# SyncE's loads in program order, head additions one VectorE operation later, and a head step inside a layer's first pair of chunks, in a Fourier-operator kernel

## The chip, the cores and the metric

The kernel runs on one core of one Trainium2 chip. The metric is the device time of one execution in microseconds, the median over the runs shown. One more execution was profiled; every duration in this document that is not called a run's time comes from such a profile.

## The reference

The input is `x`, eight images of 8 channels and 256x256 pixels. The work per image is a group norm, a Fourier neural operator of four layers with a two-matrix head, a residual addition, a second group norm, a 3x3 maximum filter and a second residual addition. Cut to what is computed:

```python
def _spectral_conv(x, w1, w2):
    xf = jnp.fft.rfft2(x).reshape(Bb, G, WID, Hh, Wf)
    lo = jnp.einsum('bgixy,gioxy->bgoxy', xf[:, :, :, :M1, :M2], w1c)
    hi = jnp.einsum('bgixy,gioxy->bgoxy', xf[:, :, :, Hh - M1:, :M2], w2c)
    return jnp.fft.irfft2(out_ft.reshape(Bb, G * WID, Hh, Wf), s=(Hh, Ww))
...
h = _gconv1x1(h, fc0_w, fc0_b)
for i in range(4):
    h1 = _spectral_conv(h, sp_w1[i], sp_w2[i])
    h2 = _gconv1x1(h, w_w[i], w_b[i])
    h = h1 + h2
    if i < 3:
        h = _gswish(h, betas[i])
h = _gswish(_gconv1x1(h, fc1_w, fc1_b), betas[3])
return _gconv1x1(h, fc2_w, fc2_b)
...
x = x + _L0_conv_ref(_gn(x), ...)
x = x + _L1_conv_ref(_gn(x))      # 3x3 maximum, border -2
```

There are 4 groups (G) of 10 channels (WID), 12 by 12 modes kept at both ends of the rows, and a hidden width of 128 per group.

## The kernel before

The state of an image, `h`, stays in SBUF as 11 chunks (NCH). A layer works on it in stages, each a Python generator that yields where work of another stage may be put in:

- `spectrum_h` (layers 1 to 3): four VectorE transposes T0 to T3 (L353), then the matmuls `p_b` (L362) and six short VectorE products into `B` (L369).
- `mix`: twelve VectorE operations, alternately a product (L390) and a sum (L393) over the spectral weights `t` (tag `sw`, two buffers, loaded by `load_sw`, L379); two subtractions and additions into `F` (L405, L406); the matmuls `p_f` (L415); and one VectorE multiply with the mask `own` that spreads the sums into `fz` (L428).
- `rows_of`: the matmuls `p_g` (L447 or L452) in three parts and copies into `zt` (L204).
- `layer`: for each chunk a `burst` of matmuls `p_z` (L523 or L526, then L529) that ScalarE turns into `h` (L534), the VectorE transposes `turn` (L477), the matmuls `p_d` (`transform`, L494) and `p_u` (`gather`, L508). Chunks go in pairs k = 0 to 5. In layer 3 there are only bursts (L536), and each chunk is stored to DRAM (L538).

The head of image b runs while the layers of image b+1 run: it is cut into 128 steps. A step is `first` (four groups of matmuls L686 and two SiLUs, L687 and L688); odd steps add a `second` (matmuls L708 that sum into a PSUM tile `acc`) and a VectorE addition of `acc` to the output rows `y` (L713, L711 where rb is 0). Each element of a yielded tuple, `(1,)` or `(1, 1)`, is one step. A yielded "tail" gives one piece of the 3x3 filter (`dilate`) of the image before. In layer 3 the spectrum and the mix of the next image's layer 0 are taken in pieces too (`start`, through `next(side)`); what is left of that mix follows after the yield "stored".

[...]the tag `one` has two slots of one bank, and `tri` two slots of three. A step's `first` takes a slot of each, and `acc`, `p_f`, `p_b` and `p_u` take one of `one`.

TensorE, VectorE and ScalarE run in the order in which the program is written (`manual_schedule`). The DMAs on SyncE's queue (SP) are placed by a planner: the 44 loads `h<-in_xp` of layer 0 (`read_x`, L542), the weights (L379), the head's `hs<-stored` (L678), the rows `y` (L701), the stores (L538) and `load_x` (L74). Until image 0 has been stored no head runs (`alone`).

Of the kernel before, what the change touches and what calls it, by code (L numbers as in the profile page):

```python
# [19 lines left out]
HW = 256  # L20
NPIX = HW * HW
G = 4
# [21 lines left out]
def fno_dilate_kernel(ctx: ExitStack, tc: tile.TileContext, a: dict, out: bass.AP):  # L44
    nc = tc.nc
    mm = nc.tensor.matmul
    PE, DVE, ACT = mybir.EngineType.PE, mybir.EngineType.DVE, mybir.EngineType.Activation

# [74 lines left out]
    nc.vector.memset(fz, 0.0)  # L123
    own = const.tile([128, NQ], F32, tag="own", name="own")
    nc.vector.memset(own, 0.0)
    for i in range(NQ):
        nc.vector.memset(own[part(i), i : i + 1], 1.0)

# [218 lines left out]
    def spectrum_h(b, l, out_):  # L347

        rows = turned.rearrange("p t f -> p (t f)")[:, : NBLK * WID * 128]
        view = rows.rearrange("p (g i k) -> p i g k", g=G, k=32)  # L350
        for g in range(G):

            nc.vector.transpose(  # L353
                rows[:, 960 * g : 960 * (g + 1)].rearrange("p (i r) -> p i r", r=32), windows(g))
            yield (1,) if g < G - 1 else (1, 1)
        p = ps_a(f"p_b_{b}_{l}")
        for k in range(2):
            for n in range(2 * NBLK):
# [16 lines left out]
        out_["bt"] = bt  # L375
# [6 lines left out]
    def mix(b, l, out_):  # L382
# [3 lines left out]
        for n in range(12):  # L386
            k, k2 = n // 4, n // 2 % 2
            pr = turned[:, 2, 1024 * k2 : 1024 * k2 + 800].rearrange("p (g m i) -> p g m i", g=G, i=WID)
            if n % 2 == 0:
                nc.vector.tensor_tensor(  # L390
                    pr, sw[k], bt[:, k2, k].unsqueeze(2).to_broadcast([128, G, 2 * WID, WID]), ALU.mult)
            else:
                nc.vector.tensor_reduce(  # L393
                    s[k2][:, k].rearrange("p g s o -> p (g s o)"),
                    pr.rearrange("p g m i -> p (g m) i"), AX.X, ALU.add,
                )
            if n == 3:
                sw.append(load_sw(l, 2))
            if l > 0:
                if n not in (2, 6, 10):  # L400
                    yield (1,)
            elif n % 2 or n > 7:
                yield (1,)
        f = sb.tile([128, 2, 3, G, WID], F32, tag="F", bufs=1, name=f"F_{b}_{l}")
        nc.vector.tensor_tensor(f[:, 0], s[0][:, :, :, 0, :], s[1][:, :, :, 1, :], ALU.subtract)  # L405
        nc.vector.tensor_tensor(f[:, 1], s[0][:, :, :, 1, :], s[1][:, :, :, 0, :], ALU.add)  # L406
        if l == 0:
            yield (1,)

        p = ps_a(f"p_f_{b}_{l}")  # L410
        sums = p[:, : 6 * WID * G].rearrange("p (o g s k) -> p s o g k", o=WID, g=G, s=2)
        for slot in range(2):
            for n, (table, part_of) in enumerate(((0, slot), (1 + slot, 1 - slot))):
                for q in range(4):
                    mm(sums[part(q), slot], fold[part(q), table, :],  # L415
                       f[part(q), part_of].rearrange("p k g o -> p o g k"), start=n == 0, stop=n == 1)
        nc.vector.tensor_copy(fz[0:32, :, :, 24], cz[:, l])
# [8 lines left out]
        if l < 2:  # L426
            nc.vector.tensor_copy(fz[0:32, :, :, 25], cz[:, 4 if l == 0 else 3])
        nc.vector.tensor_tensor(  # L428
            fz[:, :, :, : 6 * NQ].rearrange("p o g (q k) -> p (o g) q k", q=NQ),
            p[:, : 6 * WID * G].rearrange("p (n k) -> p n k", k=6).unsqueeze(2).to_broadcast([128, WID * G, NQ, 6]),  # L430
            own.unsqueeze(1).unsqueeze(3).to_broadcast([128, WID * G, NQ, 6]), ALU.mult)

    def rows_of(b, l, side):
# [3 lines left out]
        for os_ in (range(0, 4), range(4, 8), range(8, 10)):  # L437
# [16 lines left out]
            for u, o in enumerate(os_):  # L454
# [7 lines left out]
                copy(u, dst, src)  # L462
            yield (1, 1) if os_[0] == 0 or os_[0] == 8 and l < 3 else (1,)
            if l < 3:
                yield "tail"
            elif os_[0] != 4:
                next(side, None)


    def layer(b, l, out_, stored, side):  # L470
# [68 lines left out]

        def read_x(c):  # L540
            for g in range(G):
                nc.sync.dma_start(  # L542
                    h[32 * g : 32 * g + 6, c].rearrange("p f w -> p (f w)"), a["xp"][b, c, g])

        if l == 0:
            for c in range(NCH):
                read_x(c)
            wcn = sb.tile([128, 32], F32, tag="wcn", bufs=1, name=f"wcn_{b}")
            nc.vector.tensor_scalar(wcn, wc, out_["mr"][:, 1:2], None, ALU.mult)
        if l == 3:  # L550
            for c in range(NCH):
# [6 lines left out]
                if c in (0, 1, 2, 5, 6, 7):  # L558
                    yield "tail"
                next(side, None)  # L560
            return
        for k in range((NCH + 1) // 2):
# [3 lines left out]
            if k > 1:  # L566
                gather(k - 2)
            if k == 0 or alone[0]:
                turn(c)
# [94 lines left out]


    def head(b, stored, stats):
        hs, acts, box = {}, {}, {}
# [5 lines left out]
        def load_state(k):  # L673

            if k < NQ * NCH:
                j, c = k // NCH, k % NCH
                hs[k] = sb.tile([128, PIX], F32, tag="hs", bufs=4, name=f"hs_{b}_{k}")
                nc.sync.dma_start(hs[k], stored[c][:, PIX * j : PIX * (j + 1)])  # L678

        def first(n):  # L680
# [10 lines left out]
        def second(n):  # L691

            t, rb = n // 16, n % 16
            if rb == 0:
                if last:
                    y = ya[:, 1 + 2 * t : 3 + 2 * t, 1 : HW + 1]
                else:
                    y = sb.tile([128, 512], F32, tag="yp", name=f"y_{b}_{t}")
                    y = y.rearrange("p (s w) -> p s w", s=2)
                box["y"] = y  # L700
                nc.sync.dma_start(  # L701
                    y, a["x"][b].rearrange("c (p t s w) -> (c p) t s w", p=16, t=8, s=2)[:, t])
            y, acc = box["y"], ps_a(f"p_fc2_{b}_{n}")
            sums = acc.rearrange("p (s w) -> p s w", s=2)
            for i in range(2):
                act = acts.pop(n + i)
                for g in range(G):
                    mm(acc[part(g), :], w2[:, g, 15 - rb - i : 47 - rb - i], act[:, g, :],  # L708
                       start=i == 0, stop=i == 1)
            if rb == 0:  # L710
                nc.vector.scalar_tensor_tensor(y, sums, b2, y, ALU.add, ALU.add)  # L711
# [11 lines left out]

        load_state(0)
        load_state(1)
        yield
        for n in range(STEPS):
# [5 lines left out]
            yield  # L733
        second(STEPS - 2)


# [38 lines left out]

    heads, tails, count = [], [], [0]

    def step():
# [8 lines left out]
        count[0] += 1  # L787
        return True
# [5 lines left out]
    stats_of = {}  # L794
    with tc.manual_schedule(engines={PE, DVE, ACT}):
        d = {}
        for _ in start(0, d):
            pass
        for b in range(n_img):
            stored = [dram.tile([128, NQ * PIX], F32, tag=f"hs{c}", name=f"stored_{b}_{c}") for c in range(NCH)]  # L800
            ahead = {}
            for n in layers(b, stored, d, start(b + 1, ahead)):
                if n == "stored":
                    if b + 1 < n_img:
                        stats_of[b] = sb.tile([128, 8, 6], F32, tag="bn_y", name=f"bn_y{b}")
                    else:
                        stats_of[b] = spare[:, 16384:16480].rearrange("p (n s) -> p n s", s=6)
                    heads.append((b, head(b, stored, stats_of[b])))
                    next(heads[-1][1])
                    alone[0] = False  # L810
                elif n == "tail":
                    tail()
                elif heads:
                    for _ in n:
                        step()
            d = ahead
        while step():
            tail()
        for t in tails:
# [165 lines left out]
```

## Time and profile before

| | us |
|---|---|
| median of 3 runs | 3972.9 (3970.92 to 3978.73) |
| profiled execution, its own time | 3984.03 |
| its span, first to last instruction | 3982.2 |
| TensorE busy | 3689.1 |
| ScalarE busy | 2829.6 |
| VectorE busy | 2443.7 |
| mean granted TensorE clock | 0.960 |

The profiled execution took 11 us more than the median of the runs. An engine's busy time is a sum over stages with different limits, so the table says only where to look first: which wait ends last in a stage is read from the timeline of that stage. One image takes 484.6 us in the steady part: the second mix's `p_f` of two successive images start at 1430.29 and 1914.92 us.

### The profile page before, as it was taken

The numbers are of one execution on the slowest core, as the hardware profiler recorded it, in microseconds if no ns is written. First come the engines' busy times: TensorE is split into PE (matmuls) and PEld (weight loads), VectorE is DVE, ScalarE is ACT, GpSimd is POOL, SyncE is SP. The second block draws the span as 40 slices with busy tenths as digits, with TensorE's granted clock in tenths as the row PEclk, the third lists the DMA queues.
The fourth block names the chain that finished last, engine by engine and source line by source line (L and its number), as shares of the span: only waits on it lengthen the run. The fifth ranks groups of instructions, "written<-read, shape, count | busy, mean of one in ns | idle before, by whom it ended". The sixth has DMA issues, their size and how long they took to land.

```text
span 3982.2 us, 116980 instructions
## 1 busy us (share of the span) xinstructions
PE 3689.1 (93%) x53114; PEld 1427.5 (36%) x53114; DVE 2443.7 (61%) x3675; ACT 2829.6 (71%) x2923; POOL 116.9 (3%) x202
## 2 busy tenths in 40 slices
PE   5669999999999999999999999999999989999997
PEld 2334333333333333333333333333333333333222
DVE  6665665466675666756666566665666556764643
ACT  3336777767777677776777767777777767778886
POOL 1000000000000000000000000000000000000000
PEclk8879999999999999999999999999999989999998
DMA  3014111432125221261213611135112542115321
GB/s 86 15 47 173 51 41 35 164 95 63 59 85 176 62 61 57 80 212 33 63 54 94 198 36 60 56 123 167 56 43 58 163 121 59 56 44 188 110 70 47
DMA packets 114121, 344.94 MB, mean 87 GB/s; under 512 B 16040, under 2 KB 18536, under 8 KB 98200
## 3 DMA queue, kind: packets, MB, share of 16 engines
q1 hardware_dynamic: 95432, 276.32, 22.3%
q0 software_dynamic: 18192, 61.13, 4.7%
q8 instruction: 418, 6.85, 0.7%
q14 instruction: 79, 0.65, 0.1%
HBM read 213.39 MB, written 123.74 MB: 85 GB/s over the span
## 4 chain that ended last, share of the span: by engine, by line
PE 79%; DVE 11%; issue 4%; ACT 4%; DMA 3%; SPq 0%; POOL 0%; DVEq 0%; POOLq 0%; ACTq 0%
PE p_fc L686 22%; PE p_fc L708 21%; PE p_z L529 9%; PE p_d L494 7%; PE p_z L526 6%; PE p_z L523 3%; PE p_u L508 3%; PE p_b L362 2%; DVE turned L477 2%; PE p_g L452 2%; PE p_g L447 2%; PE p_f L415 2%; DVE turned L353 1%; DVE turned L390 1%; DMA t<-in_spw 1%
## 5 line engine op out<-in xcount | busy, mean ns | idle before, releaser
L688 ACT ACTIVATE act<-p_fc 128x1536 f32<-128x1536 f32 x1024 | 1491.2, 1456 | 1.4 <-PE p_fc L686 1.4
L686 PE MATMUL p_fc<-hs,c_w 32*128 32x512 f32 x8192 | 1183.1, 644 | 49.1 <-DVE y L713 22.0
L708 PE MATMUL p_fc<-act,c_w 128*32 128x512 f32 x8192 | 1003.2, 606 | 5.1 <-ACT act L687 4.7
L687 ACT ACTIVATE act<-p_fc 128x512 f32<-128x512 f32 x1024 | 615.1, 601 | 494.2 <-PE p_fc L686 479.4
L477 DVE STREAM_TRANSPOSE turned<-h 128x1024 f32<-128x1024 f32 x528 | 630.3, 1225 | 322.6 <-ACT h L534 322.4
L534 ACT ACTIVATE h<-p_z 128x512 f32<-128x512 f32 (+1 forms) x528 | 511.8, 1021 | 293.1 <-PE p_z L529 293.1
L713 DVE TENSOR_TENSOR y<-p_fc,y 128x512 f32<-128x512 f32 x392 | 268.2, 684 | 569.8 <-PE p_fc L708 569.6
L686 PEld LDWEIGHTS p_fc<-hs,c_w 32*128 32x128 f32 x8192 | 379.5, 187 | 628.4 <-ACT act L687 226.9
L708 PEld LDWEIGHTS p_fc<-act,c_w 128*32 128x32 f32 x8192 | 216.7, 110 | 733.8 <-issue 366.2
L529 PE MATMUL p_z<-c_binv,zt 32*128 32x256 f32 x5632 | 422.1, 415 | 0.0
L529 PEld LDWEIGHTS p_z<-c_binv,zt 32*128 32x128 f32 x5632 | 264.3, 191 | 318.1 <-issue 305.0
L526 PE MATMUL p_z<-h,c_wt 32*32 32x512 f32 x8448 | 353.5, 599 | 6.2 <-ACT act L687 4.1
L494 PE MATMUL p_d<-turned,c_fw 32*32 32x480 f32 (+1 forms) x9216 | 312.2, 541 | 20.9 <-DVE turned L477 20.6
L498 ACT ACTIVATE turned<-p_d 128x1440 f32<-128x1440 f32 x144 | 183.1, 1271 | 101.7 <-PE p_d L494 98.5
L536 ACT ACTIVATE h<-p_z,c_bias 128x512 f32<-128x512 f32 (+1 forms) x176 | 186.6, 1111 | 71.0 <-PE p_z L529 70.8
L204 DVE COPY zt<-p_g 128x264 f32<-128x264 f32 x300 | 161.9, 617 | 95.2 <-PE p_g L447 42.4
L494 PEld LDWEIGHTS p_d<-turned,c_fw 32*32 32x32 f32 x9216 | 129.3, 103 | 201.7 <-issue 66.8
L390 DVE TENSOR_TENSOR turned<-t,B 128x800 f32<-128x800 f32 x192 | 188.5, 982 | 20.5 <-DMA t<-in_spw 20.4
L393 DVE TENSOR_REDUCE S<-turned 128x80 f32<-128x800 f32 x192 | 189.0, 984 | 5.7
L353 DVE STREAM_TRANSPOSE turned<-zt 128x960 f32<-128x960 f32 x96 | 177.4, 1874 | 2.5
L415 PE MATMUL p_f<-F,c_fold 32*32 32x120 f32 x1024 | 62.1, 391 | 102.7 <-DVE F L405 86.9
L526 PEld LDWEIGHTS p_z<-h,c_wt 32*32 32x32 f32 x8448 | 94.1, 103 | 163.5 <-ACT act L687 59.8
(180 smaller groups left out, 1997.2 us busy)
## 6 DMA issues: line engine op xcount, KB each, us to landing
stored<-h SPq DMA_DIRECT2D x88, 1024.0 KB
hs<-stored SPq DMA_DIRECT2D x352, 256.0 KB
t<-in_spw SPq DMA_DIRECT2D x96, 400.0 KB
yin<-y_rows POOLq DMA_DIRECT2D x56, 512.0 KB, 5.0
h<-in_xp SPq DMA_DIRECT2D x352, 48.0 KB
turned<-in_xw SPq DMA_DIRECT2D x16, 1024.0 KB
y<-in_x SPq DMA_DIRECT2D x56, 256.0 KB
y_rows<-y POOLq DMA_DIRECT2D x56, 256.0 KB, 2.3
```

Source lines behind the costliest of these rows:

```text
L353: nc.vector.transpose(rows[:, 960 * g : 960 * (g + 1)].rearrange("p (i r) -> p i r", r=32), windows(g))
L390: nc.vector.tensor_tensor(pr, sw[k], bt[:, k2, k].unsqueeze(2).to_broadcast([128, G, 2 * WID, WID]), ALU.mult)
L477: nc.vector.transpose(dst[:, 2 * i : 2 * i + 2], h[:, c, 2 * i : 2 * i + 2].rearrange("p f (s x) -> p f s x", s=2))
L494: mm(banks[q][part(v % 4), : 240 * n], fw8[part(q), v, :], t[part(q), :, :, v, : NBLK * WID], start=v < 4, stop=v >= 4)
L526: mm(o, wt[part(q), l, g, :], h[part(q), c, f, :], start=True, stop=False)
L529: mm(banks[q][:, HW * s : HW * (s + 1)], zt[part(q), 2 * c + s].rearrange("p f o -> p (f o)"), binv[part(q), :], start=False, stop=s == 1)
L534: nc.scalar.activation(dst, src, AF.Silu)
L686: mm(banks[g], w1[part(g), blk, :], hs[k][part(g), :], start=True, stop=True)
L687: nc.scalar.activation(act[:, 0, :], one, AF.Silu)
L688: nc.scalar.activation(act[:, 1:4, :], tri, AF.Silu)
L708: mm(acc[part(g), :], w2[:, g, 15 - rb - i : 47 - rb - i], act[:, g, :], start=i == 0, stop=i == 1)
L713: nc.vector.tensor_tensor(y, sums, y, ALU.add)
```

## The change

- SyncE joins the engines in program order. With that, each load is written where it shall be issued. The input rows of the next image's layer 0 are loaded chunk by chunk during layer 3 (chunk c-4 after the burst of chunk c) and in the rest of the mix that follows (`rest`). The next head's first two states are loaded after chunks 8 and 10 of layer 3 (yield "ready"), the rows `y` of a block half a block ahead (`load_y`, at rb 8), and `load_x` inside the mix of layer 3, after its third operation.
- `second` no longer issues its addition: it goes on a list, and `sum_up` issues what is on the list. `sum_up` stands after each step of a tuple. After a step of a new yield "late" (in `spectrum_h`, `mix`, and the rest of the mix of layer 0) it doesn't; there the addition is issued at the head of the next step's `first`, behind the VectorE operations that lie between.
- A pair k = 0 of layers 0 to 2 has one head step between the two halves of its second transpose; for that `rows_of` ends with one step where it had two. `transform(0)` stands before the step of pair 1, where it stood behind it.
- `p_f` is summed in the order in which `F` lies in memory, and the spreading into `fz` is four copies of 32 partitions, two on VectorE and two on ScalarE. The mask `own` goes.

The diff, cut to its core:

```diff
@@ spectrum_h
                 rows[:, 960 * g : 960 * (g + 1)].rearrange("p (i r) -> p i r", r=32), windows(g))
-            yield (1,) if g < G - 1 else (1, 1)
+            yield "late"
+        yield "late"
@@ mix
-            if l > 0:
-                if n not in (2, 6, 10):
-                    yield (1,)
-            elif n % 2 or n > 7:
-                yield (1,)
+            if n not in (2, 6, 10) if l > 0 else n % 2 or n > 7:
+                yield "late"
+            if n == 2 and l == 3 and b + 1 < n_img:
+                load_x(b + 1)
...
         if l == 0:
-            yield (1,)
+            yield "late"
         p = ps_a(f"p_f_{b}_{l}")
-        sums = p[:, : 6 * WID * G].rearrange("p (o g s k) -> p s o g k", o=WID, g=G, s=2)
...
-                    mm(sums[part(q), slot], fold[part(q), table, :],
-                       f[part(q), part_of].rearrange("p k g o -> p o g k"), start=n == 0, stop=n == 1)
+                    mm(p[part(q), 120 * slot : 120 * slot + 120], fold[part(q), table, :],
+                       f[part(q), part_of].rearrange("p k g o -> p (k g o)"), start=n == 0, stop=n == 1)
...
-        nc.vector.tensor_tensor(
-            fz[:, :, :, : 6 * NQ].rearrange("p o g (q k) -> p (o g) q k", q=NQ),
-            p[:, : 6 * WID * G].rearrange("p (n k) -> p n k", k=6).unsqueeze(2).to_broadcast([128, WID * G, NQ, 6]),
-            own.unsqueeze(1).unsqueeze(3).to_broadcast([128, WID * G, NQ, 6]), ALU.mult)
+        for q in range(NQ):
+            dst = fz[part(q), :, :, 6 * q : 6 * q + 6].rearrange("p o g k -> p k g o")
+            src = p[part(q), :240].rearrange("p (k g o) -> p k g o", g=G, o=WID)
+            if q % 2:
+                nc.scalar.activation(dst, src, AF.Identity)
+            else:
+                nc.vector.tensor_copy(dst, src)
@@ rows_of
-            yield (1, 1) if os_[0] == 0 or os_[0] == 8 and l < 3 else (1,)
+            yield (1, 1) if os_[0] == 0 else (1,)
@@ layer
         if l == 0:
-            for c in range(NCH):
-                read_x(c)
+            for c in range(NCH if b == 0 else 0):
+                read_x(b, c)
...
+                if c in (8, 10):
+                    yield "ready"
+                if c > 3:
+                    read_x(b + 1, c - 4)
...
-            if k == 0 or alone[0]:
+            if alone[0]:
...
-            yield (1,)
+            if k == 1:
+                transform(0)
+            if k > 0:
+                yield (1,)
             turn(c)
-            transform(k - 1)
-            for _ in range(2 if k > 1 and pair else 1):
+            if k > 1:
+                transform(k - 1)
+            for _ in range(min(k, 2) if pair else 1):
                 yield "tail"
@@ layers
-                if l == 3 and b + 1 < n_img:
-                    load_x(b + 1)
...
-        yield from then
+        yield from rest(b, then)
@@ head
         def first(n):
+            sum_up()
...
-            if rb == 0:
...
+            if rb == 8:
+                load_y(t + 1)
...
+            sums_due.append(lambda: add(t, rb, y, sums))
@@ driver
-    with tc.manual_schedule(engines={PE, DVE, ACT}):
+    with tc.manual_schedule(engines={PE, DVE, ACT, SP}):
...
-                    for _ in n:
+                    for _ in range(1 if n == "late" else len(n)):
                         step()
+                        if n != "late":
+                            sum_up()
```

The two new helpers:

```python
    def sum_up():
        while sums_due:
            sums_due.pop(0)()
...
    def rest(b, then):
        c = NCH - 4
        for n in then:
            yield n
            if c < NCH:
                read_x(b + 1, c)
                c += 1
        for i in range(c, NCH):
            read_x(b + 1, i)
```

More of the change, by code (lines that the diff above doesn't have):

```diff
@@ L46, in fno_dilate_kernel @@
     mm = nc.tensor.matmul
-    PE, DVE, ACT = mybir.EngineType.PE, mybir.EngineType.DVE, mybir.EngineType.Activation
+    PE, DVE = mybir.EngineType.PE, mybir.EngineType.DVE
+    ACT, SP = mybir.EngineType.Activation, mybir.EngineType.SP
     const = ctx.enter_context(tc.tile_pool(name="const", bufs=1))
@@ L123, in fno_dilate_kernel @@
     nc.vector.memset(fz, 0.0)
[L124 to L127, printed above, removed]
     def softplus(t, n, name):
@@ L467, in rows_of, with read_x @@
                 next(side, None)
+    def read_x(b, c):
+        if b < n_img:
+            for g in range(G):
+                nc.sync.dma_start(h[32 * g : 32 * g + 6, c].rearrange("p f w -> p (f w)"), a["xp"][b, c, g])
     def layer(b, l, out_, stored, side):
@@ L538, in burst @@
                 nc.sync.dma_start(stored[c], h[:, c].rearrange("p f w -> p (f w)"))
[L540 to L543, printed above, removed]
         if l == 0:
-            for c in range(NCH):
-                read_x(c)
+            for c in range(NCH if b == 0 else 0):
+                read_x(b, c)
             wcn = sb.tile([128, 32], F32, tag="wcn", bufs=1, name=f"wcn_{b}")
@@ L663, in dilate_last @@
         yield
+    sums_due = []
+    def sum_up():
+        while sums_due:
+            sums_due.pop(0)()
     def head(b, stored, stats):
@@ L678, in load_state, with load_y @@
                 nc.sync.dma_start(hs[k], stored[c][:, PIX * j : PIX * (j + 1)])
+        def load_y(t):
+            if t < 8:
+                if last:
+                    y = ya[:, 1 + 2 * t : 3 + 2 * t, 1 : HW + 1]
+                else:
+                    y = sb.tile([128, 512], F32, tag="yp", name=f"y_{b}_{t}")
+                    y = y.rearrange("p (s w) -> p s w", s=2)
+                box[t] = y
+                nc.sync.dma_start(
+                    y, a["x"][b].rearrange("c (p t s w) -> (c p) t s w", p=16, t=8, s=2)[:, t])
         def first(n):
+            sum_up()
             k, blk = n // 32 * NCH + n % 32 // NBLK, n % 32 % NBLK
@@ L693, in second @@
             t, rb = n // 16, n % 16
-            if rb == 0:
[L695 to L703, printed above, removed]
+            if rb == 8:
+                load_y(t + 1)
+            y, acc = box[t], ps_a(f"p_fc2_{b}_{n}")
             sums = acc.rearrange("p (s w) -> p s w", s=2)
@@ L709, in second, with add @@
                        start=i == 0, stop=i == 1)
+            sums_due.append(lambda: add(t, rb, y, sums))
+        def add(t, rb, y, sums):
             if rb == 0:
@@ L724, in head @@
         load_state(0)
+        yield
         load_state(1)
+        load_y(0)
         yield
@@ L773, in dilate @@
             yield
-    heads, tails, count = [], [], [0]
+    heads, tails = [], []
     def step():
@@ L786, in step @@
             return step()
-        count[0] += 1
         return True
@@ L800, in fno_dilate_kernel @@
             stored = [dram.tile([128, NQ * PIX], F32, tag=f"hs{c}", name=f"stored_{b}_{c}") for c in range(NCH)]
-            ahead = {}
+            ahead, new = {}, None
             for n in layers(b, stored, d, start(b + 1, ahead)):
[L803 to L809, printed above, removed]
+                if n == "ready":
+                    if new is None:
+                        if b + 1 < n_img:
+                            stats_of[b] = sb.tile([128, 8, 6], F32, tag="bn_y", name=f"bn_y{b}")
+                        else:
+                            stats_of[b] = spare[:, 16384:16480].rearrange("p (n s) -> p n s", s=6)
+                        new = head(b, stored, stats_of[b])
+                    next(new)
+                elif n == "stored":
+                    heads.append((b, new))
                     alone[0] = False
@@ L813, in fno_dilate_kernel @@
                 elif heads:
-                    for _ in n:
+                    for _ in range(1 if n == "late" else len(n)):
                         step()
+                        if n != "late":
+                            sum_up()
             d = ahead
         while step():
+            sum_up()
             tail()
```

## Prediction

> **What bounds the kernel now.** First the page: which engine is full, and at what clock.
>
> ```profile
> PE 3689.1 (93%) x53114; PEld 1427.5 (36%) x53114; DVE 2443.7 (61%) x3675; ACT 2829.6 (71%) x2923; POOL 116.9 (3%) x202
> ...
> PEclk8879999999999999999999999999999989999998
> ```
>
> TensorE is busy for 93% of the span, so a microsecond in which it stands still, or runs at half clock, is one of the total; VectorE and ScalarE have room. Next the waits, TensorE's alone.
>
> ```profile
> PE p_f L415 <- DVE F L405: 86.9, 26, 13.1
> PE p_fc L686 <- DVE y L713: 22.0, 7, 5.7
> PE p_d L494 <- DVE turned L477: 20.6, 17, 1.4
> ...
> PE p_z L523 <- DVE wcn L549: 14.3, 7, 3.4
> ```
>
> These four are nearly all: the end of a mix (L415), a head step in the rest of layer 0's mix (L686), the first `p_d` of a layer, the first burst of layer 0. Their places are read from the timeline; here is the end of layer 2's mix, and TensorE's clock around it in windows (columns: stretch, length, busy time of PE, PEld, DVE, ACT, POOL, then the clock).
>
> ```profile
> 1550.36 0.28 DVE L405 TENSOR_TENSOR F<-S,S 128x120 f32<-128x120 f32 x1
> 1550.79 1.94 PE L415 MATMUL p_f<-F,c_fold 32*32 32x120 f32 x32 [2.13 <-DVE F L405]
> 1552.66 2.09 PE L686 MATMUL p_fc<-hs,c_w 32*128 32x512 f32 x8
> ```
>
> ```profile
> 1548.70:1552.10 3.40, 1.31 (x25) 0.92 (x29) 2.18 (x5) 1.92 (x2) 0.00 (x0) 1.00 0.84 234
> 1552.10:1555.50 3.40, 3.40 (x24) 0.88 (x20) 1.16 (x1) 0.73 (x2) 0.00 (x0) 0.51 0.04 10
> 1555.50:1558.90 3.40, 3.40 (x28) 1.36 (x21) 0.83 (x2) 2.00 (x3) 0.00 (x0) 0.99 0.30 77
> ```
>
> TensorE waits 2.13 us for F, and then runs at clock 0.51 for 3.4 us: the next `first` takes 2.09 us where 1.14 is usual. The wait costs some 1.2 us more than it shows. It stands in all 21 mixes of layers 1 to 3 that have a head beside them (images 1 to 7).
>
> The third place is a load. SyncE's and VectorE's lines at the end of one layer 3:
>
> ```profile
> 1758.40 6.12 SPq L542 DMA_DIRECT2D h<-in_xp  x4
> 1764.61 0.35 SPq L538 DMA_DIRECT2D stored<-h  x1
> ...
> 1766.19 1.13 SPq L379 DMA_DIRECT2D t<-in_spw  x1
> ...
> 1770.91 0.35 SPq L538 DMA_DIRECT2D stored<-h  x1
> ...
> 1773.22 0.99 DVE L390 TENSOR_TENSOR turned<-t,B 128x800 f32<-128x800 f32 x1 [4.17 <-DMA t<-in_spw]
> ```
>
> SyncE waits in the `h<-in_xp` loads (each needs its chunk's store landed), so chunk 10's store leaves at 1770.91 although ScalarE had finished it at 1762.35, and the weights leave at 1766.19 although the buffer was free at 1760.36 (end of the third mix operation). They land at 1773.2; VectorE stands 4.17 us, and behind it TensorE 4.81 us for the addition that frees its PSUM slot (L713).
>
> [...] `p_f`, whose moving operand steps through F and whose output lies in runs of three, takes 0.22 us for each four 120-column instructions (1.94 us for 32); `p_b` has 120 columns too and takes 0.15 (3.68 for 96). [...]
>
> **The change, part by part.** The sum is made against the profiled execution's 3984.0 us; the median of the runs is 11.1 below it.
>
> *1. Late additions, layers 1 to 3 (21 times).* I worked the stage out by hand, each engine in order, durations from the timeline: `first` 1.0 us, `second` 1.85, transpose 1.85, addition 0.6, product 1.02, sum 0.90, B 0.65, statistics 0.62, `p_b` 3.6, SiLUs 0.49 + 1.46, 0.06 between engines. Times from the `first` of step 55 (1517.22 us):
>
> | | before, worked out | before, trace | after, worked out |
> |---|---|---|---|
> | `p_b` starts | 10.88 | 10.83 | 12.00 |
> | next `first` (step 60) | 14.48 | 14.44 | 16.56 |
> | `first` of step 68 | 30.42 | 30.30 | 32.88 |
> | `p_f` starts | 33.61 | 33.57 | 34.29 |
> | `second` of step 69 ends | 38.7 | 39.72 | 39.0 |
>
> The method meets the trace within 0.15 us until the clock drops (last row). The after column has costs and a gain. The additions of steps 55 and 57 now stand behind T1 and T3: `first` of 57 and 59 find both PSUM slots taken, 0.8 + 0.6 us. The addition of step 59 stands behind `p_b`, B and the first product: step 60 waits until B has freed `p_b`'s slot, 1.0 us, and step 61 another 0.6 us. In the mix VectorE no longer stands before each addition, so the wait for F falls from 2.13 to 0.3 us, and the half clock with it. `p_f` contiguous: 8 x 0.15 + 0.15 = 1.35 us, -0.55. The four copies: VectorE two of 0.4 (the 128x240 row, 403 ns), ScalarE two of about 0.58 (128x264 takes 636 ns), overlapped 1.06 us against 1.15 for the multiply; the `second` behind gains nothing. Together -0.7 us: 21 x -0.7 = **-15**. Bounds: strict turns between the two slots give +0.5, full effect of the clock -1.7 each.
>
> *2. First pairs, layers 1 and 2 (14).* Today three bursts and an even step (1.0 us) stand before `p_d`, which waits 1.43 us for the second transpose. Now an odd step (2.9 us) stands between burst 1 and burst 2. In my working `p_d` begins 0.25 us after TensorE is free, then burst 3 waits 0.4 us for the copy out of `p_d`'s banks: pair 2 is 0.7 us earlier. 14 x -0.7 = **-10**. If the extra addition in front of the half transpose costs 0.7 us more, zero.
>
> *3. First pair of layer 0 (7).* The wait for `wcn` stays: 1.05 to 3.4 us, as one "tail" piece stands before it. The odd step that filled time before it goes behind the second burst, and the addition before `wcn` with it. Today the clock stays at half through all three bursts (10 to 14 us); a `first` and `second` between them may end that earlier. I take -1 each, **-7**; bounds +2 and -3.
>
> *4. Loads (7).* In program order the weights stand behind chunk 9's store and before the loads that wait for a store; those wait for chunks four bursts back, long landed. The weights leave at 1760.4 instead of 1766.2, need the 7 us that they take now at most, and are wanted at 1769: the wait is gone, TensorE's 1.25 to 5.7 us (21.9 in all) fall to 0.7 each, -17. Half clock followed five of these waits for 6.8 us; I count -8 of the 17 that this cost. **-25**. Zero is the bound if transport, not issue, is late. Other moved loads at nothing: `hs` waits for a slot that is free four steps earlier and is wanted six steps later (12 us and more); the weights of the next layer leave some 15 us before use; SyncE issues at 0.33 us each and idles most of the time. [...] a block's `y` load needs the store of the block before last, ten steps old.
>
> *5. Rest.* `p_f` in the other 11 mixes 11 x -0.55 = **-6**; five memsets lie beside loads.
>
> Sum -15 - 10 - 7 - 25 - 6 = -63: 3984 - 63 = 3921 against the profile, **3910** against the median.
>
> **Rivals.**
> - *SyncE becomes the bound* (slower). Today stores leave 8.5 us late in layer 3. In strict order each `hs` load stands behind a store that waits for ScalarE. If SyncE falls more than 13 us behind (20 us to the use, less 7 of transport), TensorE waits for `hs` in layer 3: at 22 us of lag 9 us, and 3 for half clock, per image, 7 x 12 = +84, part 4 gone: 3973 - 38 + 84 = 4019. Against it: no wait on `hs` shows today, and the loads that blocked SyncE move four bursts away. 10%.
> - *Held PSUM slots.* If the slots take strict turns and the clock still halves at `p_f` (1.4 us), part 1 is +1.9 x 21 = +40 instead of -15: 3965. Without the half clock 3936. The trace doesn't show which slot is taken. 22%.
> - *Loads are transport-bound.* The weights land no earlier since 1 MB of store is in front: part 4 is zero, 3935. 15%.
> - That the change doesn't do what it says: the rows of L542 and L713 would stand where they stand. Counted in the last 3%, of which 1 is slower.
>
> **How the numbers follow.** The forecast has 50%: 3910, by itself 3870 to 3940 (parts 1 and 4 at their bounds). A measurement tells 0.2%, 8 us, from no change. Faster: 50 + 15 + most of 22, and 1 = 82%; same: 5 of the slots' 22 and 1 = 6%; slower 12%, the SyncE rival, 1 of the slots' and 1 of the last. The range, 3868 to 3972, leaves out the slower cases above and some 8% below.
>
> **What would show it.** Right: no wait of `p_f` on F above 0.5 us and clock 1.00 behind it; `p_f` at 1.4 us; `first` waits on `y` in `spectrum_h` rising to about 3 us a layer; no DMA wait before L390 in layer 0's mix; stores leaving right behind ScalarE. Wrong: a wait of L686 on `hs`, half clock in `spectrum_h`, or a stage from T0 to the `second` behind `p_f` longer than 40 us.

## The result and the profile after

The changed kernel takes 3960.5 us (median of 10 runs, 3953.2 to 3971.8); the kernel before takes 3972.7 beside it (10 runs, 3964.6 to 3981.5). The ratio is 0.9967, 95% interval 0.9954 to 0.9979: about 13 us faster, where 63 were forecast. The profiled execution took 3966.3 us, its span 3964.2, 18 us below the span of before. In what follows a ratio is always to the kernel before on the same chip, and a difference of two ratios is given in microseconds by multiplying it by 3972.7; such a difference is known to about 10 us (7 for SyncE's).

First the page of the changed kernel, TensorE's busy time and its clock.

```profile
PE 3646.8 (92%) x53114; PEld 1400.4 (35%) x53114; DVE 2427.5 (61%) x3702; ACT 2865.8 (72%) x2987; POOL 117.0 (3%) x202
...
PEclk8888999999999999999999999999999999999998
```

TensorE is busy 42 us less for the same 53114 matmuls: fewer of them run at half clock (it is granted for 243 us of the span, against 323 before) and `p_f` is shorter. But the span fell by 18 only, so some 24 us of new standing have come in. TensorE's waits name them (columns: total, times, longest).

```profile
PE p_f L411 <- DVE F L402: 47.1, 24, 13.0
PE p_fc L736 <- ACT fz L428: 40.6, 28, 1.6
PE p_fc L721 <- ACT act L722: 25.7, 52, 0.8
PE p_fc L721 <- DVE B L367: 20.4, 21, 1.0
PE p_fc L721 <- DMA hs<-stored: 17.6, 5, 8.0
PE p_fc L721 <- DVE y L745: 17.3, 25, 2.0
...
PE p_z L527 <- DVE wcn L548: 12.7, 8, 3.0
...
PE p_d L498 <- DVE turned L481: 0.4, 2, 0.2
```

The wait on F fell from 86.9 to 47.1, the wait of `p_d` from 20.6 to 0.4, as forecast. In their place stand three: L736 on `fz`, 28 times 1.4 us, which the forecast had at nothing; L721 on B, on `act` and on `y`, the held slots that it had worked out (63 us in all, about 3 for each of the 21 layers); and L721 on an `hs` load, twice in image 0 (8.0 and 3.9 us) and once each in three later images (1.5 to 2.4 us). L736 is the `second` of a head step; here it is, behind layer 2's `p_f`, in the timeline.

```profile
1561.19 1.02 PE L411 MATMUL p_f<-F,c_fold 32*32 32x120 f32 x32 [0.41 <-DVE F L402]
1562.14 1.14 PE L721 MATMUL p_fc<-hs,c_w 32*128 32x512 f32 x8
1562.27 0.56 DVE L430 COPY fz<-p_f 32x240 f32<-32x240 f32 x1 [0.92 <-PE p_f L411]
1562.86 0.57 ACT L428 ACTIVATE fz<-p_f 32x240 f32<-32x240 f32 x1
1563.46 0.56 DVE L430 COPY fz<-p_f 32x240 f32<-32x240 f32 x1 [0.63 <-ACT fz L428]
1564.05 0.56 ACT L428 ACTIVATE fz<-p_f 32x240 f32<-32x240 f32 x1 [0.62 <-DVE fz L430]
1564.67 1.92 PE L736 MATMUL p_fc<-act,c_w 128*32 128x512 f32 x16 [1.38 <-ACT fz L428]
```

The first half is as forecast: 0.41 us of wait on F instead of 2.13, `p_f` 1.02 us instead of 1.94, the `first` behind it at full speed (1.14 us). Then the four copies run strictly one after the other, VectorE and ScalarE taking turns, 2.35 us from 1562.27, and the `second` waits for the last of them.

SyncE's line at the end of the layer 3 that was shown of before, then the product that wants the weights:

```profile
1765.36 0.35 SPq L542 DMA_DIRECT2D stored<-h  x1
1769.61 0.35 SPq L377 DMA_DIRECT2D t<-in_spw  x1
1770.01 1.76 SPq L472 DMA_DIRECT2D h<-in_xp  x4
1771.87 0.35 SPq L542 DMA_DIRECT2D stored<-h  x1
```

```profile
1778.19 0.98 DVE L388 TENSOR_TENSOR turned<-t,B 128x800 f32<-128x800 f32 x1
```

The `h` loads no longer hold a store up: these two leave within 0.3 us of ScalarE's end of their chunk (1765.33 and 1771.57), where one left 8.5 us late before. The weights leave 8.6 us before the product, which doesn't wait.

### The profile page after: what moved, and what is told of

It is laid out like the page before. It is cut to its first block, busy times and chain, and to the rows that moved or that the text cites. A ratio compares the mean times of both kernels' runs of the same rounds, so it can differ in the third digit from the quotient of the medians.

```text
span 3964.2 us, 116899 instructions
## 1 busy us (share of the span) xinstructions
PE 3646.8 (92%) x53114; PEld 1400.4 (35%) x53114; DVE 2427.5 (61%) x3702; ACT 2865.8 (72%) x2987; POOL 117.0 (3%) x202
## 4 chain that ended last, share of the span: by engine, by line
PE 77%; DVE 13%; issue 4%; ACT 4%; DMA 2%; SPq 0%; POOL 0%; DVEq 0%; POOLq 0%; ACTq 0%
PE p_fc L721 19%; PE p_fc L736 19%; PE p_z L533 10%; PE p_z L530 8%; PE p_d L498 7%; PE p_u L512 3%; DVE turned L350 3%; PE p_z L527 3%; PE p_b L360 2%; PE p_g L446 2%; PE p_g L451 2%; DVE turned L388 1%; DVE S L391 1%; DVE y L745 1%; ACT act L722 1%
## 5 line engine op out<-in xcount | busy, mean ns | idle before, releaser
L721 PE MATMUL p_fc<-hs,c_w 32*128 32x512 f32 x8192 | 1157.5, 636 | 92.0 <-ACT act L722 25.7
L736 PE MATMUL p_fc<-act,c_w 128*32 128x512 f32 x8192 | 1001.8, 606 | 40.6 <-ACT fz L428 40.6
L721 PEld LDWEIGHTS p_fc<-hs,c_w 32*128 32x128 f32 x8192 | 362.6, 185 | 671.5 <-ACT act L722 222.1
L736 PEld LDWEIGHTS p_fc<-act,c_w 128*32 128x32 f32 x8192 | 217.2, 110 | 758.5 <-issue 395.4
L530 PE MATMUL p_z<-h,c_wt 32*32 32x512 f32 x8448 | 363.1, 601 | 8.3 <-ACT act L722 4.1
L428 ACT ACTIVATE fz<-p_f 32x240 f32<-32x240 f32 x64 | 36.0, 563 | 150.9 <-DVE fz L430 147.8
```

The costliest lines, as they stand in the source:

```text
L530: mm(o, wt[part(q), l, g, :], h[part(q), c, f, :], start=True, stop=False)
L721: mm(banks[g], w1[part(g), blk, :], hs[k][part(g), :], start=True, stop=True)
```

## The experiments

The theory after the trace: three things cost what the change gained, (A) the four copies, (B) late additions in `spectrum_h`, which hold PSUM slots, (C) image 0's loads, which leave late in SyncE's order. The rivals of each are in the expectations. The profile lines and diffs are excerpts. All runs start from the changed kernel unless said otherwise.

**Additions in `spectrum_h` as before** (e2_spectrum_tuple).

```diff
-            yield "late"
-        yield "late"
+            yield (1,) if g < G - 1 else (1, 1)
```

> The changed kernel with the additions in spectrum_h one head step after each transpose as before (not late); mix and rows keep the late ones. Theory B (late additions hold TensorE's PSUM slots in spectrum_h: waits of the first of steps 57, 59, 60, 61 on y, act and B, 0.97 + 0.70 + 0.62 us and more per layer): p_b starts 1 us earlier and the next first 1 us more, about 1.0 to 2.0 us per layer gained, 21 layers: -20 to -40 against the changed kernel (3920 to 3940). Theory A alone (only the fz chain costs): within 6 us of 3960, the slots' stalls being given back at p_f.

Measured: 3904.1 us, ratio 0.9822 (0.9798 to 0.9846), 58 us below the changed kernel, more than B allowed itself. The timelines of TensorE and VectorE around `p_b`, the changed kernel first, then this one:

```profile
1538.48 3.72 PE L360 MATMUL p_b<-turned,c_eh_f 128*32 128x120 f32 x96
1542.27 0.76 DVE L367 TENSOR_TENSOR B<-p_b,io 128x40 f32<-128x40 f32 x6 [6.66 <-PE p_b L360]
1543.17 1.14 PE L721 MATMUL p_fc<-hs,c_w 32*128 32x512 f32 x8 [0.97 <-DVE B L367]
1543.82 0.68 DVE L745 TENSOR_TENSOR y<-p_fc,y 128x512 f32<-128x512 f32 x1
```

```profile
1510.58 3.71 PE L359 MATMUL p_b<-turned,c_eh_f 128*32 128x120 f32 x96
1510.83 0.69 DVE L744 TENSOR_TENSOR y<-p_fc,y 128x512 f32<-128x512 f32 x1 [1.33 <-PE p_fc L735]
1514.22 2.18 PE L720 MATMUL p_fc<-hs,c_w 32*128 32x512 f32 x16
1514.36 0.76 DVE L366 TENSOR_TENSOR B<-p_b,io 128x40 f32<-128x40 f32 x6 [2.83 <-PE p_b L359]
```

Above, VectorE stands 6.66 us with a finished sum to add, and adds only behind B; the next `first` stands 0.97 us for the slot. Below, the addition runs under `p_b` at 1510.83 and the `first` follows `p_b` at once. From the `first` of step 55 to `p_b` this run takes 10.79 us against 11.64, and from `p_b` to `p_f` 21.09 against 22.70, and much the same in all 21 layers. That is 2.5 us each, 52 in all. Four of the changed kernel's mixes show a half clock between `p_b` and `p_f` (24.3 us instead of 22.7); here there is none, another 6. Theory B is shown.

**No late addition anywhere** (e3_no_late): after every step `sum_up()` is called.

```diff
-                        if n != "late":
-                            sum_up()
+                        sum_up()
```

> The changed kernel with every addition right behind its product, in the mix too (no late additions anywhere); the rest stays changed. If the late additions are good in the mix and bad in spectrum_h, this stands above the kernel that has them back in spectrum_h alone (3904): p_f waits some 2.1 us for F again in 21 mixes (+1.65 to +2.1 each, the stretch from p_b to p_f back at 22.7) and the half clock follows (about 1.2 each): +35 to +65, so 3940 to 3970, near the changed kernel. If only spectrum_h matters: 3904 within 8.

Measured: 3945.5 us, ratio 0.9926 (0.9906 to 0.9947): 41 above the previous experiment, 16 below the changed kernel. So late additions are worth 41 us in the mix and cost 58 in `spectrum_h`. In layer 2 of image 3, `p_f` starts this long after the `first` of step 55:

| late in `spectrum_h` | late in the mix | `p_f` starts after | kernel |
|---|---|---|---|
| no | no | 33.54 us | this run (before: 33.57) |
| no | yes | 31.88 us | e2_spectrum_tuple |
| yes | yes | 34.35 us | changed |

TensorE waits 2.1 us for F again in this run, yet a half clock follows only 9 of the 21 mixes that have a head beside them, where it followed 19 before.

**The end of the mix as before** (e1_fz_back): `p_f` strided and one multiply by `own`.

```diff
-                    mm(p[part(q), 120 * slot : 120 * slot + 120], fold[...],
-                       f[part(q), part_of].rearrange("p k g o -> p (k g o)"), ...)
+                    mm(sums[part(q), slot], fold[...],
+                       f[part(q), part_of].rearrange("p k g o -> p o g k"), ...)
...
-        for q in range(NQ):
-            ...
-                nc.scalar.activation(dst, src, AF.Identity)
-            ...
-                nc.vector.tensor_copy(dst, src)
+        nc.vector.tensor_tensor(fz..., p..., own..., ALU.mult)
```

> The changed kernel with the end of the mix as it was: F is read strided by p_f, its output lies in runs of three, and one VectorE multiply by own fills fz. Everything else stays changed. Theory A (the four copies run one after the other, VectorE, ScalarE, VectorE, ScalarE, 2.35 us, and TensorE waits for the last: 1.38 us in 21 mixes, 1.64 in seven, about 2.5 alone): the wait of L736 on fz goes, p_f costs 1.94 us again instead of 1.02. Worth -1.4 x 28 = -39, and -7 of image 0 with its half clock, +0.9 x 32 = +29 for p_f: about -15 against the changed kernel (3945), between -25 and -5. Theory B (the copies hardly matter, the time is lost in PSUM slots held by late additions): at the changed kernel's 3960 or up to 15 above it, since p_f gets longer.

Measured: 3943.5 us, ratio 0.9927 (0.9904 to 0.9951), 16 below the changed kernel.

```profile
PE p_f L416 <- DVE F L406: 47.2, 24, 13.1
...
PE p_fc L738 <- DVE fz L429: 4.3, 21, 0.2
```

The wait on `fz` falls from 40.6 to 4.3 us, and `p_f` is back at 1.94 us, so that from `p_f` to the end of the next `second` this run takes 5.14 us and the changed kernel 5.40. The gain is theory A's number, with some luck: of the 20 us between the two profiles 9 lie in image 0, where the changed kernel's has a stretch that a half clock makes some 6 us longer. That isn't the copies' doing: e2_spectrum_tuple and e6_early_states have the copies and not the stretch, e8_combo has the stretch and not the copies.

The run also parts the half clock from `p_f`. With a `p_f` of 1.94 us and a wait of 0.4 us on F, none of the 21 mixes is followed by one: the short wait alone takes it away.

**F in the order in which it is read** (e5_f_in_order): VectorE writes F strided; `p_f` reads it contiguously and writes runs of three as before; one multiply by `own`.

```diff
-        nc.vector.tensor_tensor(f[:, 0], ...)
+        to = f.rearrange("p t o g k -> p t k g o")
+        nc.vector.tensor_tensor(to[:, 0], ...)
...
-                    mm(p[part(q), 120 * slot : 120 * slot + 120], fold[...],
-                       f[part(q), part_of].rearrange("p k g o -> p (k g o)"), ...)
+                    mm(sums[part(q), slot], fold[...], f[part(q), part_of], ...)
...
+        nc.vector.tensor_tensor(fz..., p..., own..., ALU.mult)
```

> The changed kernel with F written by VectorE in the order in which p_f reads it (strided writes), so that p_f's moving operand is contiguous, its output in runs of three as before, and one multiply by own in place of the four copies. Theory A: the wait on fz goes (-39 and -7 as in the other run); p_f stays between 1.0 and 1.9 us (which tells whether the strided moving operand or the broken output costs it): -20 to -45 against the changed kernel, 3915 to 3940. If VectorE's strided writes of F take longer than 0.28 us, each 0.1 us of that costs 3 us. Theory B: no more than 5 us from 3960.

Measured: 3923.1 us, ratio 0.9874 (0.9851 to 0.9897), 37 below the changed kernel.

```profile
1539.18 0.37 DVE L409 TENSOR_TENSOR F<-S,S 128x120 f32<-128x120 f32 x1
1539.49 1.02 PE L418 MATMUL p_f<-F,c_fold 32*32 32x120 f32 x32 [0.49 <-DVE F L408]
1540.57 1.16 DVE L431 TENSOR_TENSOR fz<-p_f,own 128x960 f32<-128x960 f32 x1 [0.98 <-PE p_f L418]
1541.78 1.92 PE L740 MATMUL p_fc<-act,c_w 128*32 128x512 f32 x16 [0.20 <-DVE fz L431]
```

`p_f` takes 1.02 us here too, though its output is broken into threes: it was the moving operand's stride that cost 0.92 us. The strided writes of F cost 0.09 us for each of two operations (0.37 us for 0.28). From `p_f` to the next `p_b`, layers 1 and 2 take 1349.1 us in all against 1365.7, 1.18 us each: the wait of 1.38 less the 0.2 that remains.

**`p_f` in two banks** (e9_two_banks): the quadrants that VectorE copies in one bank, those that ScalarE copies in another, both in a slot of the three-bank kind.

```diff
-        p = ps_a(f"p_f_{b}_{l}")
+        both = ps_tri(f"p_f_{b}_{l}")
+        p = both[:, 0, :]
...
-                    mm(p[part(q), 120 * slot : 120 * slot + 120], ...
+                    mm(both[part(q), q % 2, 120 * slot : 120 * slot + 120], ...
...
-            src = p[part(q), :240].rearrange("p (k g o) -> p k g o", g=G, o=WID)
+            src = both[part(q), q % 2, :240].rearrange("p (k g o) -> p k g o", g=G, o=WID)
```

> The changed kernel with p_f's four quadrants in two PSUM banks of a three-bank slot: 0 and 2, which VectorE copies, in one, 1 and 3, which ScalarE copies, in the other. Nothing else changes. If the order among the four copies comes from both engines reading one PSUM bank: VectorE's two and ScalarE's two run side by side, the chain falls from 2.35 to about 1.2 us and the wait of L736 on fz from 1.38 to under 0.3: -25 to -40 against the changed kernel, less whatever the three-bank slot makes a first wait. If it comes from their writing one SBUF tile (fz): the chain stays at 2.35 us, within 5 of the changed kernel or slower by the slot.

Measured: 3931.4 us, ratio 0.99 (0.9878 to 0.9922), 27 below the changed kernel, but not in the way that either side expected.

```profile
1669.22 0.56 DVE L431 COPY fz<-p_f 32x240 f32<-32x240 f32 x1 [0.93 <-PE p_f L412]
1669.81 0.57 ACT L429 ACTIVATE fz<-p_f 32x240 f32<-32x240 f32 x1
1670.41 0.58 DVE L431 COPY fz<-p_f 32x240 f32<-32x240 f32 x1 [0.64 <-ACT fz L429]
1670.80 1.93 PE L737 MATMUL p_fc<-act,c_w 128*32 128x512 f32 x16
1671.03 0.61 ACT L429 ACTIVATE fz<-p_f 32x240 f32<-32x240 f32 x1 [0.65 <-DVE fz L431]
```

The copies still take turns, 2.4 us, in two banks as in one (2.35 us), so a shared bank isn't what orders them. But the `second` now starts at 1670.80, before the last copy: it never read `fz`; it waited for `p_f`'s **PSUM slot**, one of the two one-bank slots that `p_f`, `p_b` and the sums of `second` share. Where the order does come from, the one tile `fz`, the one tile `p_f` or something else, no run tells.

**The kernel before with F in order alone** (e11_before_f): what e5_f_in_order does to F and to `p_f`'s moving operand, on the kernel before.

> The kernel before, with one edit: F written in the order in which p_f reads it, p_f's moving operand contiguous (its output stays in runs of three, the multiply by own stays). p_f falls from 1.94 to 1.02 us in 32 mixes, F's two operations grow from 0.28 to 0.37 us: 32 x (0.92 - 0.18) = -24. If p_f, [...]is part of what halves the clock (2.13 + 1.94 us before, 2.13 + 1.02 then), the half clock goes in some of the 21 mixes too, 1.2 us each: -30 to -45. If the wait alone halves the clock: -24 and no more.

Measured: 3950.4 us, ratio 0.9945 (0.9926 to 0.9965), 22 below the kernel before. The half clock behind `p_f` falls from 19 of the 21 mixes to 12, which speaks for `p_f`'s part in it; the time says no more than the 24 of the count. What the clock is worth stays open.

**The first pairs as before** (e7_pairs_back).

```diff
-            yield (1, 1) if os_[0] == 0 else (1,)
+            yield (1, 1) if os_[0] == 0 or os_[0] == 8 and l < 3 else (1,)
...
-            if alone[0]:
+            if k == 0 or alone[0]:
...
-            if k == 1:
-                transform(0)
-            if k > 0:
-                yield (1,)
-            turn(c)
-            if k > 1:
-                transform(k - 1)
+            yield (1,)
+            turn(c)
+            transform(k - 1)
...
```

> The changed kernel with the first pairs of layers 0 to 2 in the order of before (turn, burst, half step of rows before it). If the new order is worth the 17 us forecast for it (0.7 in 14 layers, 1.0 in seven): 3970 to 3980, and p_d waits 1.43 us for turned again (20 us in all). If the wait only moved elsewhere (burst 2 or 3 for its banks): within 4 of 3960. If the new order costs, since the addition in front of the half transpose delays burst 2: below 3956.

Measured: 3998.0 us, ratio 1.0048 (1.0028 to 1.0069), 32 above the changed kernel, twice the 17 forecast. The waits of this run:

```profile
PE p_d L498 <- DVE turned L481: 21.8, 17, 1.4
...
PE p_z L527 <- DVE wcn L548: 15.1, 8, 3.4
```

The first is the wait forecast. Between marks of the trace, images 1 to 7, the changed kernel stands against this one: from `p_f` to `p_b` in layers 1 and 2 1365.7 us against 1374.9 (-9, forecast -10); from layer 0's `p_f` to layer 1's `p_b` 728.4 against 747.3 (-19, forecast -7). Layer 0's first bursts leave half clock (granted 0.50) sooner in the changed kernel: in the seven images it lasts 48 us in all, 72 in this run. At half speed these 24 us would be worth some 12 of the 19, an estimate from the two traces.

**SyncE left to the planner** (e4_planner).

```diff
-    with tc.manual_schedule(engines={PE, DVE, ACT, SP}):
+    with tc.manual_schedule(engines={PE, DVE, ACT}):
```

> The changed kernel with SyncE left to the planner again; the order of the other engines is that of the changed kernel. If SyncE's written order is what took the wait of layer 0's mix away (18 us from p_f of layer 3 to p_b of layer 0 over images 1 to 7) and what put image 0's hs loads late (12 us): the first comes back, the second goes: +0 to +10, 3960 to 3970. If the moved load lines alone did both, the planner changes nothing: within 3 of 3960. If the order is worth what was forecast for it (25): 3975 to 3985.

Measured: 3975.7 us, ratio 0.9999 (0.9986 to 1.0013), 13 above the changed kernel. From layer 3's `p_f` to layer 0's, six stretches, the changed kernel takes 630.9 us, this one 651.0 and the kernel before 648.8: written order is worth 20 us there. The waits of VectorE on the weights are back in five of the six. Then 6 are lost again: layer 0's stretch up to `p_b` takes 728.4 in the changed kernel against 722.6 here. And the `hs` waits of images 1 to 7 (5.7 us in three of them) are gone, so those do come from SyncE's order.

Image 0's `hs` waits stay (7.3 and 4.2 us) although the planner places SyncE. The first `hs` load there, in this run and in the kernel before:

```profile
345.45 0.44 SPq L700 DMA_DIRECT2D hs<-stored  x1
```

```profile
318.25 0.33 SPq L678 DMA_DIRECT2D hs<-stored  x1
```

So theory C's mechanism, SyncE's order, falls for image 0. In the changed code the head opens at chunk 8 and the load leaves there, under either order; but the planner of the kernel before sent it far ahead of its place in that code, and why it no longer does so is not shown.

**Image 0's first states earlier** (e6_early_states).

```diff
-                if c in (8, 10):
+                if c in ((3, 4) if b == 0 else (8, 10)):
                     yield "ready"
```

> The changed kernel with the next head's first two states (hs 0 and 1) issued after chunks 3 and 4 instead of 8 and 10 in image 0's layer 3 only, where no head runs beside. Theory C (the loads stand in SyncE's order behind stores and x loads, so that hs lands 8.0 and 3.9 us late once): these two waits go, -8 to -12 against the changed kernel (3948 to 3952). Rival: the transfers themselves are late, or the wait moves to the weights or to y: within 3 us of 3960.

Measured: 3954.8 us, ratio 0.9951 (0.9933 to 0.9968), 6 below the changed kernel, within what the runs can't tell from zero. The trace tells more: the wait on `hs` falls from 17.6 to 4.8 us, and image 0's stretch from its layer 3's `p_f` to the next image's layer 0 `p_f` from 68.6 to 63.6 us, 5 us. The kernel before takes 56.4 there; what stays stands at the next load, the mix's third weights, for which VectorE waits 10.0 us here and 3.8 in the kernel before.

**Three edits together** (e8_combo): spectrum_h not late, F in order, image 0's states earlier.

> The changed kernel with three of the edits together: additions in spectrum_h not late, F written in the order p_f reads it with one multiply by own, and image 0's first two hs loads after chunks 3 and 4. If the three causes are separate, their gains add (57 + 37 + 6 = 100): 3855 to 3870. If they share the half clock behind the mix, the sum is smaller: 3870 to 3890.

Measured: 3861.3 us, ratio 0.9715 (0.9691 to 0.9738). The three single gains (0.0145, 0.0093 and 0.0016) from 0.9967 give 0.9713: they add.

**The same, with the third weights one operation earlier** (e10_combo_sw).

```diff
-            if n == 3:
+            if n == 2:
                 sw.append(load_sw(l, 2))
```

> The kernel that joins three edits (e8_combo), with the mix's third weights issued one VectorE operation earlier (n 2 in place of 3, where their buffer's last reader stands). In e8_combo image 0's weights left at 352.2 us, 4.9 us after that reader, and VectorE waited 9.7 us for them, TensorE 7.6. If the one place in SyncE's order puts them ahead of a store: image 0 gains 3 to 5 us and perhaps a half clock: -3 to -8 against e8_combo. If a store now waits behind them, or the transport is the limit: within 3.

Measured: 3866.1 us, ratio 0.9725 (0.97 to 0.9751), no difference from e8_combo. In image 0 the product that wants them:

```profile
345.36 0.38 SPq L380 DMA_DIRECT2D t<-in_spw  x1
```

```profile
352.57 0.99 DVE L391 TENSOR_TENSOR turned<-t,B 128x800 f32<-128x800 f32 x1 [8.93 <-DMA t<-in_spw]
```

SyncE's line, then VectorE's. The load leaves at 345.36, and VectorE starts at 352.57: 7.2 us of the 8.93 lie behind the issue, so one place in the order has little to give.

## Why the prediction was wrong

The direction and the range were right, the sum was not. The two profiles, before and changed, show where it went wrong (spans, in us; one profile each, so a few us of clock are chance):

| stretch | forecast | measured |
|---|---|---|
| part 1: in 21 mixes, from the `first` of step 55 to the end of the `second` behind `p_f` | -15 | +11 |
| image 0, up to the second image's first `p_f` | -2 | +19 |
| all else: parts 2 to 4 and seven `p_f` | -46 | -48 |
| sum | -63 | -18 |

Parts 2 to 4 came as a sum; that their sizes, by the undoing below, were off in opposite ways is luck. What failed is part 1, and the nothing that was put down for image 0. Undoing single edits from the changed kernel prices them:

| part | forecast | measured (by undoing) |
|---|---|---|
| late additions (forecast for layers 1 to 3) | -7 | +16 |
| `p_f` and the four copies | -14 | +16 |
| first pairs, all layers | -17 | -32 |
| loads, SyncE's order | -25 | -13 |
| sum | -63 | -13 |

(Part 1's -0.7 is split by its own table: `p_f` starts 0.68 later, the clock gives 1.02 (39.72 in the trace against 38.7 worked out), and from `p_f` to the end of `second` 0.38 is saved; the last, with part 5, is the second row. That the measured column meets the total so well is partly luck: each entry is known to 7 to 11 us, what one undoing gives depends on what else is changed, and the moved load lines, which stay when the planner places SyncE, are in no row.)

**The four copies** are the step that failed outright: "The four copies: VectorE two of 0.4 (the 128x240 row, 403 ns), ScalarE two of about 0.58 (128x264 takes 636 ns), overlapped 1.06 us against 1.15 for the multiply; the `second` behind gains nothing." ScalarE's size was right (0.56), VectorE's was 0.56 instead of 0.4, and the overlap did not exist: 2.35 us. Why the copies take turns stays open; that it isn't a shared bank is shown by e9_two_banks (2.4 us in two banks). The last half-sentence let the `second` hang on the end of that work; with the right duration it would have read "loses 1.2 us, 28 times", +33. That size is shown: with the same fast `p_f` and one multiply (e5_f_in_order) the stretch from `p_f` to the end of the `second` takes 4.22 us, with the copies 5.40. `p_f` itself gave more than forecast, 0.92 against 0.55.

**Late additions.** The hand-worked table was good: `p_b` at 12.00 (trace 11.64), the next `first` at 16.56 (16.33), the `first` of step 68 at 32.88 (32.80), `p_f` at 34.29 (34.35). The step "the wait for F falls from 2.13 to 0.3 us, and the half clock with it" held too: no half clock follows, and e1_fz_back shows that the short wait is enough for that. What it left out is that the shorter `p_f` alone takes 7 to 10 of these 19 half clocks away (9 stay in e3_no_late, 12 in e11_before_f). Beside that `p_f`, the late additions' later start, 0.68 by the table and 0.81 by trace, 17 us in 21 layers, has less clock to set against it. Four mixes got a new half clock between `p_b` and `p_f`, 6 us, which the forecast did not have. The table also held the better kernel: "0.8 + 0.6", "1.0" and "another 0.6" in `spectrum_h` against 1.8 in the mix; I added the two instead of asking what each was worth alone.

The rival of **held slots** named the right mechanism, and its 3965 lies near the 3960 measured, but for another reason: it needs a half clock that stays at `p_f`, 1.4 us a mix. None follows `p_f` in the 21 mixes now; in its place stand the copies, 1.38 us, so the nearness is luck. **SyncE as the bound** did not come: stores leave on time (the two shown within 0.3 us). Its sign, a head step that waits for `hs`, did, but outside image 0 it is worth 5.7 us.

**First pairs.** Part 2 was right (-10, measured -9). Part 3 was -7, "I take -1 each", bounds +2 and -3; undoing gives -2.7 each, inside the bounds, and by the estimate above more than half of that is the half clock.

**Loads.** -25 was forecast for the waits and the half clock behind them; the six stretches from layer 3's `p_f` to layer 0's gave -20 (against e4_planner; -18 against the kernel before). Half clock followed four of the six waits, not five; in the changed kernel it comes there three times and for 3.4 us instead of 6.8. What the sum left out are the 6 us that layer 0, against e4_planner, loses again behind it. And "Other moved loads at nothing: `hs` waits for a slot that is free four steps earlier" failed: in image 0 no head runs beside, the head is opened at chunk 8, and TensorE waited 8.0 and 3.9 us. Of the 19 us that image 0 lost, 12 lie from its layer 3's `p_f` on; e6_early_states gets 5 of them back. Some 6 are the stretch at half clock that comes and goes between runs.

## What to carry to other kernels

Here a PSUM slot was held until its last reader ended, so lengthening the copies out of it (2.35 us instead of a multiply of 1.16), or moving an addition behind other work, charged the matmul that took that slot next (1.38 us of wait for the `second`, 0.97 for the `first` behind `p_b`), even where it read none of the data; ask of each late reader who needs its buffer next. Delaying an operation paid where its engine had more urgent work standing behind it, in the mix (41 us), and cost where the engine had nothing else to do, in `spectrum_h` (58 us). Before counting copies on two engines as overlapped, look for a timeline in which such copies do overlap; putting the order into the producer's write (0.18 us here) bought the same fast matmul (1.02 us) without them. And price the parts of a change one by one: e8_combo, without the copies and the late additions of `spectrum_h` and with two loads moved, runs at 3861 us, 100 below the change as a whole.

## What the runs showed of the hardware

`p_f` paid for reading its moving operand with a stride, not for a PSUM output broken into runs of three: its 32 matmuls of 120 columns take 1.94 us with both (before, e1_fz_back), 1.02 with neither (changed), and 1.02 with the broken output alone (e5_f_in_order).

The half clock behind `p_f`, in the 21 mixes of layers 1 to 3 with a head beside them:

| wait for F | `p_f` at full clock | half clock follows | kernel |
|---|---|---|---|
| 2.1 us | 1.94 us | 19 | before |
| 2.1 and 2.2 us | 1.02 us | 9 and 12 | e3_no_late, e11_before_f |
| 0.4 us | 1.94 us | 0 | e1_fz_back |
| 0.4 us | 1.02 us | 0 | changed |

Behind a wait of 2.1 to 2.2 us the half clock followed 19 of the 21 mixes with the longer `p_f`, 9 and 12 with the shorter, so `p_f`'s length matters beside the wait. Why it does was not tested.
